# Where the second mamba block's small work stands: three edits to the order of a four-stage kernel

## The chip, the core and the metric

The kernel runs on one core of a Trainium2 chip. Its engines work side by side, each through its own list of instructions in order: TensorE (PE in the profile, with its weight loads as PEld), VectorE (DVE), ScalarE (ACT), GpSimd (POOL) and SyncE (SP), which only issues transfers. They meet through semaphores: an instruction that waits holds up everything behind it on its engine. The metric is the device time of one execution in microseconds (us). Lower is better.

## The reference

Two sequences of 1024 tokens with 512 channels go through four sub-layers, each followed by a residual sum and a layer norm:

```python
x = layernorm(x + L0_attn(x))   # mamba: in-projection, causal conv, recurrence over tokens, gate, out-projection
x = layernorm(x + L0_ffn(x))    # one 512x512 linear product, scaled, with tanh norm clipping
x = layernorm(x + L1_attn(x))   # gated linear recurrence: two branches, conv, two gates, scan, out-projection
x = layernorm(x + L1_ffn(x))    # SiLU-gated FFN with integer weights, 2048 wide
```

The part of the first sub-layer that matters here is this one. `dt` and `dA` have one value per head and token, `B` and `C` 16 values per token:

```python
conv = conv_b + sum(xpad[:, k:k+l] * conv_w[:, k] for k in range(4))
x, B, C = split(silu(conv))
dt = softplus(dt + dt_bias);  dA = exp(dt * -exp(A_log))
h = h * dA_t + (dt_t * x_t) outer B_t;   y_t = h . C_t
```

## The kernel before

The data are float32 (the linear product and the FFN split them into two pieces). The 2048 tokens are cut into four blocks of 512 (`TB`), and each block into four chunks of 128.

**Mamba.** For a block, `head` transposes the tokens (L232, copied out of PSUM at L241 by ScalarE and L243 by VectorE), multiplies out B, C and dt (`pbc`, L353), and prepares their convolution, which the function `mix` finishes: three taps on VectorE (`causal_conv`, L264) and a SiLU on ScalarE (L312). For blocks 1 to 3 `by_rows` then computes softplus and the decays on 64 rows (bias L440, softplus L208 to L219, decays L442 to L450), sends them to DRAM (`since`, `decays`) and transposes the row values back (`ptk` L455, `tk` L456). The constants of the decays, `by_hj`, come by two small transfers on POOL's queue (L108), and `exponents` (L192 to L196) turns A_log into three columns of it.

`opening` is block 0's projection, in an order written out by hand for TensorE, VectorE and ScalarE. It ends with the taps of the last channels (`started_in_psum`, L325) and their SiLU (L329), after which `by_token` transposes the result (`pxt`, L632) and the recurrence starts. `recur` runs the four chunks: products `py` (L655, L663), state `pst` (L673), sums on VectorE (L680, L687, L694), and `pxt`, `dtx` (L634) for the next chunk. `weave` puts steps of other generators between the chunks by a plan: here block 0's gate products (`g`, L336 `pg`, SiLU L705) and steps of block 1's head (`ahead`). Then `gate` (L713 and its squares L715) and block 1's `project` follow: its taps (L264), its copies of the decay rows into PSUM (`pl`, L529), its scans (L535), among the out-projection of the block before (`conclude`, L728). SP loads block 1's decay rows (`L<-decays`) once block 0's last chunk has read the tile `L`.

**The rest.** `linear(b)` is the second sub-layer for one block: transposes, split into two pieces (ScalarE L236, VectorE L237), products `po` (L909), scaling (L913), norms (L915 to L931), update and layer norm (the last on POOL, L257). `branches(b)` begins the third: transposes with copies by ScalarE (L241), products `p` (L960), taps (L982, L264). `linear(2)` and `linear(3)` are woven into `branches(0)`. `recurrence` computes the gates and the scan (L1009 to L1031), `project_back` the out-projection `po` (L1037), its bias `r` (L1042), and the sum into the tokens (POOL, L1043). The FFN (L1111 to L1134) fills the rest.

Outside the hand-written stretches a scheduler sets each engine's order from program order, priorities and its own model of durations. `tc.keep_in_program_order` holds one instruction where the program has it; `tc.high_priority()` lets instructions go ahead of others that are ready.

## Time and profile before

| | us |
|---|---|
| median of three runs | 1141.38 |
| lowest and highest run | 1140.03 and 1142.83 |
| the profiled execution: its time | 1140.83 |
| its span, from the first to the last instruction | 1139.0 |
| TensorE busy in the span | 1116.2 |
| VectorE, ScalarE, POOL busy | 677.6, 466.1, 357.8 |

The span by stages, from the chain that ended last and the timeline: block 0's opening to about 71 us, its recurrence to 97, block 1's projection to 162, blocks 2 and 3 to 431, the linear layer and the first branches to 505, the gated recurrence to 768, then the FFN to the end. The chain follows, from the last instruction backwards, what each step waited for; a row of the timeline is start, duration, engine, line, operation, and in brackets how long the engine had been idle and what ended that. Matmul rows overlap a little at their ends, since the profile models those.

### The profile page before, as it was taken

To read this page: it belongs to the slowest core of one execution; us is meant where nothing else is said; L and a number is where in the kernel's file an instruction comes from. 1 tells how busy PE (TensorE), PEld (TensorE's weight loads), DVE (VectorE), ACT (ScalarE), POOL (GpSimd) and SP (SyncE) were. 2 spreads that over 40 slices of the span, in tenths; PEclk is the share of its full clock that TensorE was granted. 3 is DMA by queue.
4 is the path that set the end of the run, shared out by engine and by line. 5 is a ranking of instruction groups with operands and counts; after the bars stand their busy time and mean duration, and the time that the engine had idled before them with its cause. 6 is when DMAs were issued, how large, how long until landed. Compare 5 with 4: busy or idle time off the path is not lost.

```text
span 1139.0 us, 12263 instructions
## 1 busy us (share of the span) xinstructions
PE 1116.2 (98%) x4610; PEld 681.3 (60%) x4610; DVE 677.6 (59%) x1226; ACT 466.1 (41%) x714; POOL 357.8 (31%) x347
## 2 busy tenths in 40 slices
PE   8999999999999999999999999999999999999996
PEld 5455445545544655654444444448888888888885
DVE  5997895696769676862707237083328765225224
ACT  3352634453453233566654372543223223223224
POOL 1547461573348240556123212237501001001000
PEclk9999999999999999999999999999999999999999
DMA  9004002401210047112000000003601001000001
GB/s 325 13 16 167 1 1 90 167 0 39 111 71 0 38 173 207 75 47 74 1 1 0 1 0 1 0 1 121 184 1 38 1 1 37 1 1 10 28 1 40
DMA packets 32732, 59.22 MB, mean 52 GB/s; under 512 B 11841, under 2 KB 12641, under 8 KB 30105
## 3 DMA queue, kind: packets, MB, share of 16 engines
q1 hardware_dynamic: 31464, 57.94, 14.6%
q8 instruction: 38, 0.62, 0.2%
q10 hardware_dynamic: 976, 0.39, 0.1%
q14 instruction: 30, 0.24, 0.1%
q0 software_dynamic: 224, 0.02, 0.0%
HBM read 49.47 MB, written 8.68 MB: 51 GB/s over the span
## 4 chain that ended last, share of the span: by engine, by line
PE 84%; DVE 10%; ACT 4%; issue 1%; DMA 1%; SPq 0%; DVEq 0%; ACTq 0%
PE pgu L1111 21%; PE p L960 17%; PE po L1134 10%; PE pg L336 9%; PE px L336 7%; PE po L728 6%; PE po L1037 4%; PE py L663 3%; DVE acc L264 2%; PE po L909 2%; DVE L L535 2%; PE pxt L632 1%; PE pt L232 1%; DVE xc L713 1%; PE py L655 1%
## 5 line engine op out<-in xcount | busy, mean ns | idle before, releaser
L1120 DVE SCALAR_TENSOR_TENSOR h<-pgu,L_ffn_up_scale,sg 128x512 f32<-128x512 f32 x64 | 47.9, 749 | 147.7 <-PE pgu L1111 143.5
L336 PE MATMUL px<-xT,w_in 128*128 128x512 f32 x256 | 114.6, 597 | 0.0
L550 POOL TENSOR_TENSOR L<-L,gm 128x512 f32<-128x512 f32 x64 | 93.5, 1490 | 66.9 <-DVE bdec L545 29.3
L728 PE MATMUL po<-w_out,xc 128*128 128x512 f32 x256 | 112.5, 593 | 2.1 <-DVE L L535 2.1
L336 PE MATMUL pg<-xT,w_in 128*128 128x512 f32 x256 | 113.5, 594 | 0.0
L960 PE MATMUL p<-xT,w 128*128 128x512 f32 x256 | 112.1, 592 | 1.4 <-ACT xT L241 1.4
L960 PE MATMUL p<-cv,w 128*128 128x512 f32 x256 | 111.0, 592 | 0.0
L1134 PE MATMUL po<-wd,hh 128*128 128x512 f32 x256 | 101.3, 396 | 0.0
L1111 PE MATMUL pgu<-wF__4423,wg 128*128 128x512 f32 x256 | 101.2, 396 | 0.0
L1134 PE MATMUL po<-wd,hl 128*128 128x512 f32 x256 | 101.0, 394 | 0.0
L1111 PE MATMUL pgu<-lo__4424,wg 128*128 128x512 f32 x256 | 100.7, 394 | 0.0
L1111 PE MATMUL pgu<-lo__4424,wu 128*128 128x512 f32 x256 | 100.7, 393 | 0.0
L1111 PE MATMUL pgu<-wF__4423,wu 128*128 128x512 f32 x256 | 100.7, 393 | 0.0
L1118 ACT ACTIVATE sg<-pgu,L_ffn_gate_scale 128x512 f32<-128x512 f32 x64 | 44.1, 689 | 132.9 <-PE pgu L1111 132.9
L1126 ACT CAST hh<-h 128x512 fp32r<-128x512 f32 x64 | 39.7, 621 | 117.6 <-DVE h L1120 117.4
L728 PEld LDWEIGHTS po<-w_out,xc 128*128 128x128 f32 x256 | 48.4, 190 | 63.1 <-issue 55.5
L960 PEld LDWEIGHTS p<-cv,w 128*128 128x128 f32 x256 | 48.4, 190 | 59.8 <-issue 58.6
L960 PEld LDWEIGHTS p<-xT,w 128*128 128x128 f32 x256 | 48.4, 190 | 58.8 <-issue 55.3
L336 PEld LDWEIGHTS px<-xT,w_in 128*128 128x128 f32 x256 | 47.6, 190 | 57.6 <-issue 56.7
L1241 POOL TENSOR_TENSOR x<-x,r 128x512 f32<-128x512 f32 x12 | 15.2, 1295 | 206.1 <-DVE r L1240 206.1
L336 PEld LDWEIGHTS pg<-xT,w_in 128*128 128x128 f32 x256 | 47.3, 190 | 54.2 <-issue 53.3
L264 DVE SCALAR_TENSOR_TENSOR acc<-xpad,cols,acc 128x512 f32<-128x512 f32 x72 | 67.5, 941 | 18.5 <-ACT acc L306 14.8
(279 smaller groups left out, 1934.5 us busy)
## 6 DMA issues: line engine op xcount, KB each, us to landing
L<-decays SPq DMA_DIRECT2D x12, 1024.0 KB, 8.3
x_mid<-x SPq DMA_DIRECT2D x4, 1024.0 KB, 3.9
x<-x_mid SPq DMA_DIRECT2D x4, 1024.0 KB, 7.2
st<-in_L_ffn_gate_w_dram SPq DMA_DIRECT2D x8, 512.0 KB, 4.7
st<-in_L_ffn_up_w_dram SPq DMA_DIRECT2D x8, 512.0 KB, 3.9
st<-in_L_ffn_down_w_dram SPq DMA_DIRECT2D x8, 512.0 KB, 3.7
x<-_attn_hidden_states_dram SPq DMA_DIRECT2D x3, 1024.0 KB, 16.6
out_dram<-x SPq DMA_DIRECT2D x3, 1024.0 KB, 4.3
```

The lines of the kernel that those rows point to most:

```text
L264: nc.vector.scalar_tensor_tensor(acc, xpad[:, k : k + TB], w[:, k : k + 1], acc, ALU.mult, ALU.add)
L336: nc.tensor.matmul(pm[:n, :], w_in[:, k, lo : lo + n], xT[:, k, :], start=(k == 0), stop=(k == NK - 1),)
L550: nc.gpsimd.tensor_tensor(L[:, h, :], L[:, h, :], st["gm"], ALU.mult)
L663: nc.tensor.matmul(pys[i][hh * HD : (hh + 1) * HD, q, :], dtx[q][:, 2 * i + hh, :], L[:, h, s], start=(first and q == 0), stop=(q == 1), s ...
L728: nc.tensor.matmul(po, xc[:, m, j * P : (j + 1) * P], w_out[:, m, :], start=(m == 0), stop=(m == NX - 1),)
L960: nc.tensor.matmul(pm, w1[:, i, k, m * P : (m + 1) * P], rhs[:, k, :], start=(k == 0), stop=(k == NK - 1),)
L1037: nc.tensor.matmul(po, y[:, k, j * P : (j + 1) * P], w1[:, 4, k, :], start=(k == 0), stop=(k == NK - 1),)
L1111: nc.tensor.matmul(pm, w[g][:, k, cols], x[:, k, :], start=(k == 0 and x is pieces[0]), stop=(k == NK - 1 and x is pieces[-1]),)
L1118: nc.scalar.activation(sg, pgu[0], AF.Silu, scale=gs[:, m : m + 1])
L1120: nc.vector.scalar_tensor_tensor(h, pgu[1], us[:, m : m + 1], sg, ALU.mult, ALU.mult)
L1126: nc.scalar.copy(hh, h)
L1134: nc.tensor.matmul(po[j], x[:, j * P : (j + 1) * P], wd[m // GK][:, m % GK, :], start=(m == 0 and x is h[0]), stop=(m == NF - 1 and x is h ...
```

## The change

Four edits, and line numbers in the text stay those of the kernel before:

1. `opening` no longer runs `mix` of block 1 (its second `next(coming)` goes). The plan of block 0's recurrence becomes (2, 2, 1, 2) over (ahead, g, ahead, g, g, g, ahead): `mix` stands after chunk 0, the decays after chunk 1, `ptk` after chunk 3. The first tap of that `mix` is held in program order.
2. `by_rows` of block 1: the bias L440 is issued ahead of `exponents` and is held in program order; `exponents` is no longer held.
3. The first step of `linear(2)`, its transposes and split, is issued ahead of `branches(0)` rather than after its transposes.
4. The bias `r` of `project_back` (L1042) is issued at high priority.

```diff
-    def causal_conv(acc, xpad, w):
+    def causal_conv(acc, xpad, w, pinned=False):
         for k in range(3):
-            nc.vector.scalar_tensor_tensor(
+            tap = nc.vector.scalar_tensor_tensor(
                 acc, xpad[:, k : k + TB], w[:, k : k + 1], acc, ALU.mult, ALU.add
             )
+            if pinned and k == 0:
+                tc.keep_in_program_order(tap)
...
-        def rest():
-            causal_conv(acc[:n, :], xpad[:n, :], w)
+        def rest(pinned=False):
+            causal_conv(acc[:n, :], xpad[:n, :], w, pinned)
...
-            mix()
+            mix(b == 1)
...
+        bias, _, end, rA, rN = (by_hj[:, i : i + 1] for i in range(5))
+        shifted = nc.vector.tensor_scalar(z, z, bias, None, ALU.add)
         if b == 1:
-            exponents(*(by_hj[:, i : i + 1] for i in range(1, 5)), pinned=True)
-        bias, _, end, rA, rN = (by_hj[:, i : i + 1] for i in range(5))
-        nc.vector.tensor_scalar(z, z, bias, None, ALU.add)
+            tc.keep_in_program_order(shifted)
+            exponents(*(by_hj[:, i : i + 1] for i in range(1, 5)))
...
         later.pop(0)()
-        next(coming)
         for conv in later:
...
-            turns = (ahead, g, g, ahead, g, g)
-            weave(recur(b, H, st), (next(steps, None) for steps in turns), (2, 2, 1, 1))
+            turns = (ahead, g, ahead, g, g, g, ahead)
+            weave(recur(b, H, st), (next(steps, None) for steps in turns), (2, 2, 1, 2))
...
-                    nc.vector.tensor_tensor(r, po, bout, ALU.add)
+                    with tc.high_priority():
+                        nc.vector.tensor_tensor(r, po, bout, ALU.add)
...
-            weave(branches(0, st), itertools.chain(linear(2), linear(3)), (1,) * 8)
+            rest = itertools.chain(linear(2), linear(3))
+            next(rest)
+            weave(branches(0, st), rest, (0,) + (1,) * 7)
```

In the changed program, as built, the instructions stand as follows on each engine; where nothing is said, the order is the one before.

- VectorE at the start: after the first copy L243 come three instructions of block 1's `exponents` (L192, L193, L194 on `by_hj`, the first waiting for the A_log transfer), then the second copy L243. ScalarE: after its first copy L241 comes that group's `exp` (L195), then its second copy L241.
- VectorE in block 0: all taps L325, then `dtx` and chunk 0; `mix`'s three taps after chunk 0's work; L440 to L216 after chunk 1's; the rest of the decays among chunk 2's work; `tk` (L456) among the products L713. `ptk` is TensorE's last instruction before block 1's projection.
- TensorE at `branches(0)`: the 16 transposes of block 2 before the 16 of block 0. ScalarE: three of linear(1)'s squares L915, a split copy L236, the fourth L915, a second L236, the norm L919, two more L236, table load and tanh L923, and then the four copies L241; before it was four L915, L919, L923, two L236, four L241, two L236.
- VectorE in `project_back` of blocks 0 to 2: the four `r` stand together after the last scan L1025 and before the last L1031; before, one stood ahead of that L1031 and three behind it.

## The prediction

> **What bounds the kernel now.** I read the page's busy shares first, then TensorE's waits, then the timeline around each wait.

> ```profile
> PE 1116.2 (98%) x4610; PEld 681.3 (60%) x4610; DVE 677.6 (59%) x1226; ACT 466.1 (41%) x714; POOL 357.8 (31%) x347
> ```

> TensorE is busy 98%: all four edits together can win at most its idle 22.8 us (1139.0 - 1116.2). TensorE's list of waits names the ones in reach:

> ```profile
> PE pxt L632 <- ACT xc L329: 2.4, 1, 2.4
> PE po L728 <- DVE L L535: 2.1, 2, 1.1
> PE po L1037 <- DVE r L1042: 1.7, 1, 1.7
> ...
> PE p L960 <- ACT xT L241: 1.4, 1, 1.4
> ...
> PE po L909 <- DVE wd L237: 0.8, 1, 0.8
> ...
> PE pt L232 <- POOL xpad L976: 0.5, 1, 0.5
> ```

> The first is the opening's end (edits 1, 2), the fourth and sixth stand ahead of branches(0) (edit 3), the third is the bias (edit 4). Now the timeline of the start:

> ```profile
> 4.97 0.56 POOL L108 DMA_DIRECT2D by_hj<-in_L_attn_A_log_dram  x1
> ...
> 8.72 0.69 DVE L243 COPY xT<-pt 128x512 f32<-128x512 f32 x1 [0.18 <-PE pt L232]
> ...
> 9.05 1.93 PE L353 MATMUL pbc<-xT,w_bc 128*48 128x256 f32 x16
> ...
> 12.49 7.13 PE L336 MATMUL px<-xT,w_in 128*128 128x512 f32 x16
> ```

> From 12.49 to 51.5 the rows of TensorE touch each other: what starts late there stays late.

> **Part A, the start: +2.6 us.** Unpinned, block 1's exponents stand between VectorE's two copies L243 and wait for the A_log transfer. The DMA table prices it:

> ```profile
> by_hj<-in_L_attn_A_log_dram POOLq DMA_DIRECT2D x1, 0.2 KB, 6.5
> ```

> Issued at 4.97, it lands at 11.47. L192 to L194 take 0.44 (their twins on 128x16 ran from 9.33 to 9.77). So the second L243 runs 11.9 to 12.6 instead of 8.72 to 9.41; queued behind it, ScalarE's L195 (0.20) and its second copy L241 (0.59) end at 12.7. The product pbc has four k steps of 0.48 and needs a copy for each: the last two end at 13.6 instead of 11.0. Everything up to 51.5 moves by 2.6. Bounds: 0, if it landed before 8.5; 3.3, if it took the 7.2 of the slowest POOL row.
> [...] The row says 6.5, and it decides.

> **Part B, the wait at 71: -1.9.** Block 1's work between the last taps cost VectorE 4.98 (chain pieces from 61.43 to 69.68: L264 1.22, 0.66, 0.66; L440 0.20; L208 0.20; L210 0.12; L211 0.86; L212 1.06). Without it the last tap ends at 70.42 - 4.98 + 2.6 = 68.0, but its SiLU L329 is queued on ScalarE behind the gate L705 of a pg that ended at 67.98 and now ends at 70.6: 70.6 + 0.6 + 0.63 gives 71.85 against TensorE's arrival at 71.35. A wait of 0.5 to 0.6 is left of 2.44, so A and B together are +0.7 at the first py.

> **Part C, where the work goes: +1.6 instead of that +0.7.** The mix (three taps of 0.76) fits into the gap after chunk 0, whose next py comes only after a pg. The decays start after chunk 1's dtx, 85.37 + 0.65 = 86.0. Block 2's rows price them: L440 to the first L216 3.1, six L216 1.87, L217, L219, L442, L443, L444 1.5, exp, scan and memset 0.8, together 7.3. Among them lie chunk 2's L694 1.4, L680 0.35, two L687 1.2 and two dtx 1.3, together 4.2; alternating saves about 0.8 of the waits of one step for the last. So VectorE reaches chunk 3's sums at 86.0 + 7.3 + 4.2 - 0.8 = 96.7, where it now waits for TensorE until 95.38:

> ```profile
> 95.38 0.79 DVE L694 TENSOR_TENSOR xc<-xc,py 128x256 f32<-128x256 f32 x2 [2.32 <-PE py L663]
> ...
> 99.12 9.06 DVE L713 TENSOR_TENSOR xc<-xc,g 128x512 f32<-128x512 f32 x6
> ```

> It is +1.3 there, and `tk` (0.29), now among the L713, makes 1.6. From here the chain of waits runs L713, square L715, ScalarE's xpad and acc, taps L264, scans L535, to the pxt at 161.91, by VectorE and ScalarE alone; TensorE idled 1.05 + 1.02 + 0.65 in that stretch, waiting for them. So 1.6 passes on whole. Bounds: +1.0, if alternating hides 1.4; +3.7, if the slow rows of 61 to 92 return (L212 1.14 for 0.28, L216 0.90 for 0.31, L687 1.67 for 1.06, which add 2.1).
> Covered: the row transfers. `decays` is written about 14 us later, lands near 100, and SP's four loads of L (1 MB each, 4 MB at some 340 GB/s, 12 us) end at 112.5; ScalarE first reads them at 122.54 (pl, L529). Were that cover gone, the excess would count whole. `cdec` goes ahead of them on SP; `ptk` waits for nothing late.

> **Part D, the linear step: +1.0.** Block 2's transposes need no layer norm, so the 0.45 on POOL goes. But look at ScalarE:

> ```profile
> 464.37 1.28 ACT L923 ACT_TABLE_LOAD   x1
> 465.66 0.20 ACT L923 ACTIVATE f<-v 128x4 f32<-128x4 f32 x1
> 465.77 1.05 ACT L236 CAST wu<-pt 128x512 fp32r<-128x512 f32 x2
> 466.72 2.06 ACT L241 COPY xT<-pt 128x512 f32<-128x512 f32 x4
> ```

> TensorE's p L960 waits 1.41 for the first L241. Now all four L236 (0.51 each) stand ahead of it, two of them before the fourth L915: third L915 from 462.63 (0.76), L236, L915 0.73, L236, L919 0.20, two L236, table load 1.28, tanh 0.20, with small gaps 467.87; the first L241 ends at 468.4, not 467.3. It is +1.05. VectorE's wd wait at 496 (0.79) may shrink: part of linear(2)'s split is done earlier, but a layer norm on POOL and the tap behind it start later. I take +1.0; bounds +0.3 (that wait gone) and +1.3.

> **Part E, the bias: 0.** TensorE's 1.66 ends with the first `r`, which frees its bank; it follows the same scan:

> ```profile
> 752.81 1.28 DVE L1025 TENSOR_TENSOR_SCAN hs<-al,last,gx 128x512 f32<-128x512 f32 x1
> 754.01 0.67 DVE L1042 TENSOR_TENSOR r<-po,L_attn_b_out 128x512 f32<-128x512 f32 x1
> 754.59 0.68 DVE L1031 TENSOR_TENSOR y<-y,hs 128x512 f32<-128x512 f32 x1
> ```

> The other three `r` now stand ahead of the last L1031: y comes 3 x 0.62 later, at 757.1. The first po (3.43) needs it for its last quarter, near 757.5; these 0.4 cover it. Bounds 0 and +0.5, if the scan runs long.

> **The sum.** A + B + C is +1.6 in the end, D +1.0, E 0: +2.6. The span becomes 1141.6, the profiled run's 1140.83 becomes 1143.4; that run lay 0.55 below the median, so on the median 1141.38 it is **1144.0**, 0.23% more. By the bounds: low, with A at 0 the 1.6 becomes -1.0, and with D at +0.3 the sum is -0.7: 1140.7; high, A +0.7, C +2.1, D +0.3 and E +0.5 more: 1147.6.
> [...] Part A leaves TensorE idle for 2.6; the profile's 2.44 at 69 left the granted clock at 1.00. [...]

> **The rivals.** A difference under 0.3% (3.4 us) can't be told from none.
> *Slower: the decays overrun chunk 3.* Place: VectorE from 86 to 97, price one for one from where its sums L694 come after TensorE's py (96.0). For it: the slow rows above, all beside POOL's L638, and w_out's scaling (L773, 92.31 to 98.1) is there too. Against: block 2's same chain shows none of them. +2.1: 1146.1. Chance 0.27.
> *By_hj is early enough, or its delay is lost.* For it: VectorE has idle rows before 52. Against: TensorE has none from 12.49, and skips, issued a microsecond earlier, released POOL only at 10.68. C's 1.6 becomes -1.0, D +1.0: 1141.4. Chance 0.13.
> *The edits do what they aim at.* The waits of 1.9, 0.45 + 1.41 and 1.66 go, 5.4 in all: 1136.0. Against: the queues of A, D and E. Chance 0.10.
> *My forecast*, 1144.0: 0.50; its own range is 1142.4 to 1146.0, and 0.14 of it lies above 1144.8, the bound of slower.

> **How the numbers follow.** Slower 0.27 + 0.14 = 0.41; within 0.3% 0.36 + 0.13 = 0.49; faster 0.10. The range, 1139.5 to 1147.5, leaves out the last rival and a tail of the first.

> **What would show it.** A: an idle of about 3 us ahead of L192 on VectorE, released by by_hj, and px at 15.1. B: the wait at pxt under 1. C: VectorE's first L694 of chunk 3 over 1.5 us later than 95.38 with no wait for py before it, and the pxt of block 1 near 163.5. D: p L960 waits over 3 us for L241. E: po L1037 still waits 1.7 for r. I am wrong if L192 waits under 1 us, or if pxt of block 1 comes before 161.9.

## The result and the profile after

| | before | after |
|---|---|---|
| median, six runs of each (us) | 1141.87 | 1146.94 |
| lowest and highest | 1140.03 and 1142.83 | 1144.95 and 1148.12 |
| profiled execution: span | 1139.0 | 1144.8 |
| its mean granted TensorE clock | 0.998 | 0.995 |

The ratio is 1.0045, with a 95% interval from 1.0032 to 1.0058: slower by about 5.1 us. That is inside the range of the prediction, 2.9 us above its number, and on the side of slower, which had 0.41 against 0.49 for no change. Line numbers of the changed kernel are shifted (L336 is L338, L353 is L355, L632 L636, L634 L638, L687 L691, L694 L698, L713 L717, L915 L919, L960 L964, L1031 L1035, L1037 L1041, L1042 L1047); each experiment's rows have its own.

The page of the changed kernel, its busy line and the row of the granted clock in 40 slices:

```profile
PE 1120.3 (98%) x4610; PEld 682.8 (60%) x4610; DVE 678.0 (59%) x1226; ACT 462.6 (40%) x712; POOL 358.6 (31%) x347
...
PEclk8999999999999999999999999999999999999999
```

The same 4610 matrix products took TensorE 1120.3 us, where they took 1116.2. Work that got longer without getting more is a sign to look at the clock, and its first slice is below 9. Then TensorE's waits, in us in total, times, and the longest:

```profile
PE p L964 <- ACT xT L241: 2.7, 1, 2.7
PE pbc L355 <- DVE xT L243: 2.5, 1, 2.5
...
PE po L1041 <- DVE r L1047: 1.7, 1, 1.7
...
PE py L667 <- DVE dtx L638: 0.9, 2, 0.8
...
PE pxt L636 <- DVE dtx L638: 0.4, 1, 0.4
PE po L1041 <- DVE y L1035: 0.3, 1, 0.3
```

The wait of 2.4 at the first `pxt` is down to 0.4. In its place stand a new one of 2.5 at `pbc`, 0.9 at `py`, 0.3 at `y`, and the one at `p` is 2.7 for 1.4. The bias's 1.7 is untouched. Now the start in the timeline (start, duration, engine, line, operation, idle time before it and what ended it):

```profile
7.74 0.69 DVE L243 COPY xT<-pt 128x512 f32<-128x512 f32 x1 [5.04 <-PE pt L232]
...
11.45 0.14 DVE L192 TENSOR_SCALAR by_hj<-by_hj 64x1 f32<-64x1 f32 x1 [3.01 <-DMA by_hj<-in_L_attn_A_log_dram]
...
11.77 0.67 DVE L243 COPY xT<-pt 128x512 f32<-128x512 f32 x1
...
12.50 1.12 PE L355 MATMUL pbc<-xT,w_bc 128*48 128x256 f32 x8 [2.48 <-DVE xT L243]
...
15.17 6.19 PE L338 MATMUL px<-xT,w_in 128*128 128x512 f32 x8
```

VectorE stood 3.01 us before L192 for A_log, the second copy L243 behind it came at 11.77 instead of 8.72, and `px` began at 15.17 instead of 12.49. But eight `px` rows then took 6.19 us, while sixteen took 7.13 before. The table by stretches shows why; its columns are the stretch, its length, the busy time (and number of rows) of PE, PEld, DVE, ACT and POOL, the granted clock, the DMA share and GB/s:

```profile
10.02:12.50 2.48, 0.00 (x1) 0.01 (x1) 1.02 (x6) 0.63 (x2) 0.37 (x2) 1.00 0.92 348
...
13.20:13.40 0.20, 0.20 (x4) 0.00 (x0) 0.00 (x0) 0.00 (x0) 0.00 (x0) 0.96 1.09 430
13.40:13.60 0.20, 0.20 (x2) 0.00 (x0) 0.00 (x0) 0.00 (x0) 0.00 (x0) 0.50 1.19 471
14.00:20.00 6.00, 5.92 (x15) 3.13 (x16) 3.83 (x17) 1.77 (x6) 0.35 (x2) 0.50 1.03 402
...
20.20:20.40 0.20, 0.20 (x2) 0.06 (x1) 0.17 (x2) 0.00 (x0) 0.00 (x0) 0.97 1.05 389
```

The clock was 1.00 through the idle 2.48 us, fell to 0.50 at 13.39 and came back at 20.21: 6.8 us at half speed, soon after the idle time, and never in the kernel before, whose clock is 1.00 in the whole of that stretch.

Following the same instruction in both traces gives the account. How much later than before each began, in us:

| instruction | later by | what is new since the row above |
|---|---|---|
| `px`, first row | 2.68 | the stall at `pbc` |
| `pl` at 51.5 before | 5.17 | 2.49, the halved clock |
| `py` of block 0, first row | 3.16 | -2.01, the wait at `pxt` |
| sums L698 of chunk 3 | 6.06 | +2.90, VectorE late |
| end of the gate L717 | 2.50 | -3.56, faster gate products |
| `pxt` of block 1, its last | 4.18 | +1.68, taps that wait for POOL |
| `p` L964, 505.59 before | 5.04 | +0.86, the linear step |
| first `pgu`, 768.17 before | 5.59 | +0.55, the bias |
| the last instruction | 5.8 | +0.2, behind the last row of every computing engine; not followed up |

### The profile page after: what moved, and what is told of

The parts are those of the page before. It is cut to its first block, busy times and chain, and to the rows that moved or that the text cites. A ratio compares the mean times of both kernels' runs of the same rounds, so it can differ in the third digit from the quotient of the medians.

```text
span 1144.8 us, 12265 instructions
## 1 busy us (share of the span) xinstructions
PE 1120.3 (98%) x4610; PEld 682.8 (60%) x4610; DVE 678.0 (59%) x1226; ACT 462.6 (40%) x712; POOL 358.6 (31%) x347
## 4 chain that ended last, share of the span: by engine, by line
PE 83%; DVE 9%; ACT 4%; issue 1%; POOL 1%; DMA 1%; DVEq 0%; ACTq 0%; POOLq 0%
PE pgu L1119 21%; PE p L964 17%; PE po L1142 10%; PE pg L338 9%; PE px L338 8%; PE po L732 6%; PE po L1041 3%; PE py L667 2%; PE po L913 2%; DVE acc L264 2%; DVE L L540 1%; PE pxt L636 1%; PE pt L232 1%; PE py L659 1%; DVE st L251 1%
## 5 line engine op out<-in xcount | busy, mean ns | idle before, releaser
L338 PE MATMUL px<-xT,w_in 128*128 128x512 f32 x256 | 117.1, 607 | 0.0
L964 PE MATMUL p<-xT,w 128*128 128x512 f32 x256 | 111.8, 592 | 2.7 <-ACT xT L241 2.7
L732 PE MATMUL po<-w_out,xc 128*128 128x512 f32 x256 | 112.5, 593 | 1.8 <-DVE L L540 1.8
L338 PE MATMUL pg<-xT,w_in 128*128 128x512 f32 x256 | 113.5, 594 | 0.0
L964 PE MATMUL p<-cv,w 128*128 128x512 f32 x256 | 111.0, 592 | 0.0
L964 PEld LDWEIGHTS p<-xT,w 128*128 128x128 f32 x256 | 48.4, 190 | 60.8 <-issue 56.0
L964 PEld LDWEIGHTS p<-cv,w 128*128 128x128 f32 x256 | 48.4, 190 | 59.8 <-issue 58.6
L338 PEld LDWEIGHTS px<-xT,w_in 128*128 128x128 f32 x256 | 48.5, 194 | 59.0 <-issue 57.5
L338 PEld LDWEIGHTS pg<-xT,w_in 128*128 128x128 f32 x256 | 47.3, 190 | 54.2 <-issue 53.3
L264 DVE SCALAR_TENSOR_TENSOR acc<-xpad,cols,acc 128x512 f32<-128x512 f32 x72 | 68.0, 948 | 18.4 <-ACT acc L308 12.2
```

The source lines that it names most:

```text
L264: tap = nc.vector.scalar_tensor_tensor(acc, xpad[:, k : k + TB], w[:, k : k + 1], acc, ALU.mult, ALU.add)
L338: nc.tensor.matmul(pm[:n, :], w_in[:, k, lo : lo + n], xT[:, k, :], start=(k == 0), stop=(k == NK - 1),)
L732: nc.tensor.matmul(po, xc[:, m, j * P : (j + 1) * P], w_out[:, m, :], start=(m == 0), stop=(m == NX - 1),)
L964: nc.tensor.matmul(pm, w1[:, i, k, m * P : (m + 1) * P], rhs[:, k, :], start=(k == 0), stop=(k == NK - 1),)
```

## The experiments

Times are medians; a ratio is to the kernel before, run beside it, with its 95% interval. "Edits 1 and 2 held" means them with block 1's `exponents` kept in program order.

| run | what it is | median us | ratio (interval) | `px` from | `pxt` of block 1 | granted clock of its executions |
|---|---|---|---|---|---|---|
| e1_pinned | all four edits, `exponents` held | 1142.13 | 1.0009 (1.0 to 1.0018) | 12.49 | 160.32 | 0.994 to 0.998 |
| e2_fill | the changed kernel, 18 products in the stall | 1146.44 | 1.0049 (1.0035 to 1.0063) | 16.94 | 164.80 | 0.994 to 0.998 |
| e2b_fill9 | the same with 9 | 1145.42 | 1.0031 (1.002 to 1.0043) | 15.62 | 164.06 | 0.994 to 0.998 |
| e5_block | edits 1 and 2 held | 1139.68 | 0.9991 (0.9982 to 1.0) | 12.45 | 160.31 | 0.997 to 0.998 |
| e6_scale | e5_block, scaling of `w_out` moved | 1138.43 | 0.9972 (0.9962 to 0.9982) | 12.43 | 159.21 | 0.997 to 0.998 |
| e8_best | e6_scale, `exponents` earlier | 1138.92 | 0.9977 (0.9968 to 0.9985) | 13.11 | 159.87 | 0.997 to 0.998 |
| e3_linear | the kernel before, edit 3 | 1142.0 | 1.0009 (1.0 to 1.0018) | 13.01 | 161.55 | 0.995 to 0.998 |
| e10_lin | e6_scale, edit 3 | 1140.01 | 0.9993 (0.9984 to 1.0001) | 13.15 | 159.94 | 0.994 to 0.998 |
| e11_linfill | e10_lin, 9 products ahead of `p` | 1139.78 | 0.9989 (0.998 to 0.9998) | 12.97 | 159.73 | 0.997 to 0.998 |
| e4_bias | e5_block, edit 4 | 1141.05 | 0.9995 (0.9986 to 1.0004) | 12.76 | 161.18 | 0.997 to 0.998 |
| e12_copy | e6_scale, copies for `p` ahead | 1147.56 | 1.0058 (1.0045 to 1.0071) | 13.26 | 160.03 | 0.991 to 0.995 |

The granted clock is a mean over the whole execution. It includes the kernel's end: TensorE's last product ends at 1130.1 in the profile of the kernel before and at 1135.7 in the changed kernel's, and the clock is 0.50 from 1135.01 to the end at 1139.0, and from 1139.78 to the end at 1144.8. In the profiles with no other loss that alone makes 0.998 or 0.997; one window of half clock among the products (1.7 us lost, see below) takes off another 0.0015. So 0.996 or less tells of a loss among the products, while 0.997 leaves it open: e3_linear's profiled execution reads 0.997 and has one.

Where nothing was done to the start, `px` began between 12.43 and 13.26, since the first tokens land a little earlier or later (the transposes that wait for them go on at 7.30 in e6_scale and at 8.02 in e10_lin, and `px` begins 5.13 later in both); differences under 0.8 us between two kernels are therefore read between two instructions of a trace, not from the medians.

**The start: stall, and clock.** First, without the float of `exponents`:

```diff
-            exponents(*(by_hj[:, i : i + 1] for i in range(1, 5)))
+            exponents(*(by_hj[:, i : i + 1] for i in range(1, 5)), pinned=True)
```

> All four edits, but block 1's exponents are held in program order again, so that nothing waits for the A_log transfer at the start. Theory (the start cost a stall of 2.7 us and then a halved TensorE clock worth another 2.5): px starts at 12.5 again, the granted clock stays 1.00 from 13 to 21 us, and the whole 5.2 us go: about 0.2 us from the kernel before, 5.2 under the changed kernel. Rival (only the stall belongs to the start; px is slow for another reason): the first px rows stay near 0.77 us each and 2.7 us go, which leaves about 2.5 us more than before.

`px` began at 12.49 again, the clock stayed at 1.00, and `pl` stood at 51.52, 0.01 from its old place: the whole 5.2 us belong to these three floated instructions. In the profiled pair the theory's number came out, 0.2 us over the kernel before (spans 1139.2 and 1139.0). The median was 1.4 us over it; what may make up the difference stands below, at edit 3.

That run takes the stall and the clock away together. To part them, TensorE was kept busy while the stall stayed:

```diff
                     xT[:, k, i * half : (i + 1) * half], start=(k == 0), stop=(k == NK - 1),
                 )
+            if b == 0 and k == 1:
+                for _ in range(18):
+                    nc.tensor.matmul(early[:, :P], ident, ident, start=True, stop=True)
```

> The changed kernel, with 18 small products of the identity into the unused bank of the warm-up put between the two halves of the pbc product, where TensorE waits 2.5 us. The stall stays (VectorE still waits for A_log), TensorE is busy through it. Theory (idling brought the clock down): the granted clock stays 1.00, px starts near 15.0 with rows of 0.45 us, the shift at 51 us is 2.7 in place of 5.2, and the time falls by 2.5 us against the changed kernel. Rival (the clock has nothing to do with the idle time): the clock is 0.50 from 13.4 to 20.2 us as before and the time does not move, or is longer by what the products delay pbc.

The clock stayed at 1.00 and `px` ran at 0.45 us a row, but the products took 4.29 us, not 2.5: the filling outlasted the stall, `px` began at 16.94, and the time shows nothing. So once more with `range(9)`:

> As the run with 18 products, with 9: each took 0.24 us on TensorE there, so 18 outlasted the stall and moved px to 16.94; 9 end near 12.3, before the second half of pbc can start at 12.5. Theory (idling brought the clock down): the granted clock is 1.00 throughout, px starts at 15.1 with rows of 0.45 us, the shift at 51 us is 2.7, and the time is 2.5 us under the changed kernel, some 2.6 us over the kernel before. Rival (the stall costs 5 us by itself): as the changed kernel, some 5 us over.

In that run's timeline of TensorE:

```profile
9.84 1.07 PE L355 MATMUL pbc<-xT,w_bc 128*48 128x256 f32 x8
10.84 2.27 PE L361 MATMUL early<-ident 128*128 128x128 f32 x18
13.04 1.07 PE L355 MATMUL pbc<-xT,w_bc 128*48 128x256 f32 x8
...
15.62 7.13 PE L338 MATMUL px<-xT,w_in 128*128 128x512 f32 x16
```

and in its table of stretches, at the start and near edit 3:

```profile
14.00:20.00 6.00, 5.43 (x21) 2.82 (x20) 3.36 (x15) 2.69 (x7) 0.35 (x2) 1.00 1.03 404
...
468.00:474.00 6.00, 3.82 (x6) 1.75 (x7) 5.09 (x15) 3.56 (x7) 0.00 (x0) 0.76 0.49 175
474.00:480.00 6.00, 6.00 (x22) 3.91 (x22) 5.26 (x15) 2.88 (x5) 0.18 (x1) 0.96 0.00 0
```

Sixteen `px` rows take the 7.13 us of the kernel before, and the clock is 1.00 where it was 0.50. `px` began 3.13 late (the tokens landed later in this execution, where the transposes go on at 8.16, for 7.27 in the changed kernel, and the products kept the second half of `pbc` to 13.04, where its copy was there at 12.40) and `pl` 3.14: nothing is lost behind the stall, where the changed kernel lost 2.49. But this profile alone doesn't part theory and rival: with the tokens late, TensorE would have stood idle only from 10.91 to some 12.46 without the products, 1.55 us, and that might have left the clock alone. The executions part them in part: the changed kernel's six have mean clocks of 0.992 to 0.995, while of the twelve with products eight have 0.996 or more. The median is 1.5 us under the changed kernel's, not 2.5; `px` began 0.45 later than there, which takes part of it, and this profile has a second low stretch, at 468, behind edit 3's wait at `p`.

What settles it lies in all the profiles together. Within each one, the clock changes only at times that are whole multiples of 3.413 us apart: in the changed kernel's profile 6.83 from the fall to the rise and 1119.57 from there to the fall at the end, 2 and 328 times 3.413; in e12_copy's 10.24, 40.96 and 3.42, which is 3, 12 and 1 times. So it goes by windows of that length here, and they lie differently in each execution: counted from its start, the first whole one begins at 1.79 in the kernel before, at 3.14 in the changed kernel and at 2.28 in e12_copy. The table has TensorE's idle time within one window and the granted clock of the next one:

| run | wait in it | window from | idle in it, us | clock in the next |
|---|---|---|---|---|
| e12_copy | `pt`, for POOL | 452.84 | 2.80 | 0.50 |
| e2b_fill9 | `p` | 467.69 | 2.49 | 0.50 |
| the changed kernel | `pbc`, 2.48 | 9.97 | 2.48 | 0.50 |
| e2_fill | `p` | 468.78 | 2.17 | 0.50 |
| e3_linear | `p`, 2.75 | 463.67 | 2.16 | 0.50 |
| e12_copy | `po`, for `wd` | 504.04 | 2.02 | 0.50 |
| e1_pinned | `p`, most of 2.72 | 462.06 | 1.73 | 1.00 |
| the kernel before | `r`, 1.66 | 752.72 | 1.66 | 1.00 |
| the changed kernel | `p`, 2.73 in two windows | 467.36 and 470.77 | 1.29 and 1.44 | 1.00 |
| the kernel before | `pxt`, 2.44 in two windows | 66.64 and 70.05 | 1.31 and 1.14 | 1.00 |

The six with 0.50 are all the falls that the thirteen profiles have before TensorE's last product; 1.73 is the most idle time that any window there had without one. So the six windows with 2.02 us or more were each followed by half a clock, those with 1.73 or less never, and the two waits of over 2.4 that an edge split nearly in half did nothing. In these profiles idle time brings the clock down, and the rival falls; in the changed kernel's profile all of the stall lay in one window.

**Edits 1 and 2 without that cost.** The kernel before with edits 1 and 2 held, none of edits 3 and 4:

> The kernel before with edits 1 and 2 alone (mix and decays kept behind the taps), and block 1's exponents held in program order. Theory (tap relief of 1.9 us, of which VectorE's overload in chunks 2 and 3 gives back 1.0 by block 1's pxt): pxt of block 1 comes near 161.0, 0.9 us before its 161.91, and the time is 0.9 us under the kernel before. Rival (the overload costs its full size, 2.9 us at chunk 3's sums, since nothing later absorbs it): pxt of block 1 near 162.9, 1.0 us slower.

`pxt` of block 1 came at 160.31, 1.6 us earlier than before, and the time is 1.1 us less. `py` came 2.04 earlier (69.41 for 71.45), and of this only 0.44 was given back. The rival, an overload at its full size, falls. Yet VectorE's overload itself is there: the sums of chunk 3 begin 26.25 us after the first `py`, for 23.93 before. In the changed kernel it reads, on VectorE and POOL (POOL's row L721 in a window of its own, 104.8 to 107.4, so that its first sum stands alone):

```profile
95.38 5.68 POOL L777 TENSOR_SCALAR w_out<-w_out,cols 128x512 f32<-128x512 f32 x8
95.46 0.77 DVE L691 SCALAR_TENSOR_TENSOR H<-H,over 128x128 f32<-128x128 f32 x1
...
97.78 0.69 DVE L447 TENSOR_SCALAR work<-turn,by_hj 64x128 f32<-64x128 f32 x1
...
98.99 0.81 DVE L448 TENSOR_SCALAR work<-work,by_hj 64x128 f32<-64x128 f32 x1
...
99.12 1.75 PE L667 MATMUL py<-L,dtx 128*64 128x128 f32 x28 [0.78 <-DVE dtx L638]
...
101.44 0.75 DVE L698 TENSOR_TENSOR xc<-xc,py 128x256 f32<-128x256 f32 x2
...
104.84 2.49 DVE L717 TENSOR_TENSOR xc<-xc,g 128x512 f32<-128x512 f32 x4
105.20 3.26 POOL L721 TENSOR_TENSOR sums<-sums,sq 128x512 f32<-128x512 f32 x1 [4.13 <-ACT sq L719]
...
119.57 1.54 DVE L264 SCALAR_TENSOR_TENSOR acc<-xpad,cols,acc 128x512 f32<-128x512 f32 x2 [2.52 <-POOL xpad L306]
```

Several rows beside POOL's scaling of `w_out` take two to three times their usual 0.30 to 0.34 (L691) and 0.28 to 0.34 (L447, L448); others there, L217 and L219, keep their 0.28. TensorE's `py` waits for `dtx`, and the sums are late. Then the gate gives most of it back. In the kernel before, POOL's sums ran beside five of its last six products, and these took 1.75 each:

```profile
99.48 8.15 POOL L717 TENSOR_TENSOR sums<-sums,sq 128x512 f32<-128x512 f32 x5 [1.35 <-ACT sq L715]
```

In the changed kernel POOL stood still from 101.06 to 105.20, waiting for the late squares; two products had it idle beside them, and the next four kept their 0.68 too (2.49 for four, which overlap a little). Three of these ran beside POOL's first sum, and here POOL lost the time: that sum took 3.26, where the later ones took 1.26 to 1.60. Only the last two products took 1.55 and 1.75. Why POOL gave way there and VectorE before is not shown. The gate ends early, until POOL's sums, also late, hold up the `xpad` rows and with them the next taps (2.52). To test that the scaling makes the rows slow, it was moved to follow chunk 0:

```diff
+            def scale():
+                for m in range(NX):
+                    tc.keep_in_program_order(nc.gpsimd.tensor_scalar(
+                        w_out[:, m, :], w_out[:, m, :], normw[:, m : m + 1], 1.0,
+                        ALU.mult, ALU.mult
+                    ))
+                yield
-            turns = (ahead, g, ahead, g, g, g, ahead)
-            weave(recur(b, H, st), (next(steps, None) for steps in turns), (2, 2, 1, 2))
-            for m in range(NX):
...
+            scaled = scale()
+            turns = (scaled, ahead, g, ahead, g, g, g, ahead)
+            weave(recur(b, H, st), (next(steps, None) for steps in turns), (3, 2, 1, 2))
```

> Edits 1 and 2 with block 1's exponents held, and POOL's scaling of w_out moved from behind the whole recurrence to behind chunk 0 (about 80 to 86 us), where VectorE has little to do; to be read against the run with edits 1 and 2 alone. Theory (the slow decay rows of chunk 2 and 3, L216 at 0.79 and L447 to L449 at 0.6 to 0.8, are slow because POOL scales w_out beside them): they fall to 0.2 to 0.35, chunk 3's first sums come 2 to 2.5 us earlier and wait for TensorE again, and block 1's pxt comes up to 1.0 us earlier. Rival (POOL's sums of squares set block 1's taps, and these start when the gate's squares do): rows fall, but pxt of block 1 moves by less than 0.3.

```profile
74.91 6.66 POOL L776 TENSOR_SCALAR w_out<-w_out,cols 128x512 f32<-128x512 f32 x8
...
90.75 0.34 DVE L691 SCALAR_TENSOR_TENSOR H<-H,over 128x128 f32<-128x128 f32 x1
...
92.28 0.27 DVE L447 TENSOR_SCALAR work<-turn,by_hj 64x128 f32<-64x128 f32 x1
...
94.56 0.75 DVE L698 TENSOR_TENSOR xc<-xc,py 128x256 f32<-128x256 f32 x2
...
112.69 2.34 DVE L264 SCALAR_TENSOR_TENSOR acc<-xpad,cols,acc 128x512 f32<-128x512 f32 x3 [2.52 <-POOL xpad L306]
```

With the scaling at 74.91, L691 takes 0.34 and L447 0.27; the mix's three taps, now beside it, take 3.61 for 2.97, in time that VectorE had to spare. Some L216 stay slow (1.07 and 0.79, at 88.2 and 89.5, beside POOL's L642). Against the run with edits 1 and 2 held, the sums of chunk 3 come 1.10 earlier (2 to 2.5 were expected), POOL's sums end 1.09 earlier and `pxt` of block 1 comes 1.10 earlier: what VectorE gains there passes on one for one, and the theory's 1.0 at `pxt` holds. The rival would have had under 0.3. This is the fastest kernel of the study, 0.28% under the kernel before (interval 0.18% to 0.38%).

Then block 1's `exponents` were issued right behind the first layer's own, on top of this:

> The run with w_out's scaling moved, and block 1's exponents issued right behind the first layer's own, where VectorE stands idle for 2.9 us at 9.9 (they wait for A_log until 11.4 and have nothing urgent behind them until 12.8). Theory: no stall at the start, px at 12.5, and 0.5 us less on VectorE among the decays: between 0 and 0.5 us under the run with the scaling moved, some 1.5 us under the kernel before. Rival (the wait for A_log holds up z and the softplus behind it): px or its taps come later, and it is slower than that run.

It gained nothing: from `px` to `pxt` of block 1 it took 146.76 us, the run before it 146.78. Its median is 0.5 higher, and its `px` began 0.7 later; in this profile the first copy L243 already came at 8.46 (7.84 before), so the tokens were late, and the floated rows, at 13.47, had no part in it.

**Edit 3, the linear step.** Alone on the kernel before:

> The kernel before with edit 3 alone (the first linear step ahead of the branches). Theory (ScalarE's four split copies now stand before the four copies that p waits for): p waits 2.7 us for the copy in place of 1.4, POOL's 0.45 goes, and by the end the time is 0.7 to 0.9 us more. Rival (the earlier split pays it back at the wd wait, 0.8 us): 0 to 0.1 us more.

`p` waited 2.75 and POOL's 0.45 was gone, as in the changed kernel, whose ScalarE shows the queue:

```profile
467.43 0.57 ACT L236 CAST wu<-pt 128x512 fp32r<-128x512 f32 x1
...
468.52 0.57 ACT L236 CAST wu<-pt 128x512 fp32r<-128x512 f32 x1
...
469.09 1.07 ACT L236 CAST wu<-pt 128x512 fp32r<-128x512 f32 x2
470.18 1.28 ACT L927 ACT_TABLE_LOAD   x1
...
471.59 2.03 ACT L241 COPY xT<-pt 128x512 f32<-128x512 f32 x4
```

From the first of these transposes to the first `p` of the convolved branch, 52.46 us passed; 50.82 before. That is 1.64, more than 0.9: in this execution the granted clock was 0.92 from 462 to 468 and 0.79 from 468 to 474. The median is 1.2 over the kernel before. So edit 3 was put on the quieter base of the run with the scaling moved, and then the idle time was filled:

> The run with w_out's scaling moved, with edit 3 (the first linear step ahead of the branches) added; its base has no idle time of TensorE over 1.7 us, and its runs lie within 0.9 us of each other. Theory (edit 3 costs its wait, and in a part of the executions a lower clock behind it, by where the idle 2.7 us fall against the clock's windows): 0.9 us over the base in executions with a granted clock of 0.998, and about 1.7 us more in others with 0.996 or less; median 0.9 to 2.6 over the base, spread over 2 us. Rival (only the wait counts): 0.9 us over the base, spread as in the base.

```diff
                 xT = transposed(rp, b, X, by_act=True)[0]
+                if b == 0:
+                    spare = bank("spare")
+                    for _ in range(9):
+                        tc.keep_in_program_order(
+                            nc.tensor.matmul(spare[:, :P], ident, ident, start=True, stop=True)
+                        )
                 yield
```

> As the run with edit 3 added, with 9 small products of the identity into an unused bank (2.1 us) behind the branches' transposes, where TensorE waits 2.7 us for ScalarE's copy. Theory (the idle time lowers the clock): the wait stays as time, the granted clock stays 1.00 between 450 and 485 us, the spread shrinks to that of the base, 0.9 us over the base. Rival (the clock falls for another reason, the copies' or the products' own): the spread stays over 2 us.

In both the same stretch took 51.65, 0.80 over the base's 50.85. Without the filling the runs spread over 3.3 us (1139.29 to 1142.61): eight of twelve with a mean clock of 0.998 and spans from 1137.4 to 1138.4, four with 0.994 to 0.997 and spans up to 1140.7. With it the wait left to TensorE is 0.70, every run has 0.997 or 0.998, and they spread over 1.1 us (1139.29 to 1140.38):

```profile
462.98 2.17 PE L982 MATMUL spare<-ident 128*128 128x128 f32 x18
465.86 3.70 PE L969 MATMUL p<-xT,w 128*128 128x512 f32 x8 [0.70 <-ACT xT L241]
```

Useless work made the kernel steadier, and no slower (medians 1139.78 and 1140.01). This pair is the cleaner test of the filling: 2.6 of the 2.7 us would have lain in one window (from 463.26), and with 0.70 of it left idle the clock stayed at 1.00. In e10_lin's own profile an edge split the wait into 1.41 and 1.29, and the clock stayed up without help; its four slower executions were not profiled. The theory holds in kind. In size the median of e10_lin rose by 1.6 over the base, of which the trace gives 0.8 to the wait and 0.7 to `px`, which began that much later in the profiled execution; the base was timed in another batch, where the kernel before read 1141.54 for 1140.94 here, so the 1.6 is rough. The first experiment fits: it kept edit 3, and only four of its eleven runs had 0.998.

The other way about, ScalarE's copies for `p` ahead, by high priority for the branches' transposes:

```diff
-                xT = transposed(rp, b, X, by_act=True)[0]
+                with tc.high_priority():
+                    xT = transposed(rp, b, X, by_act=True)[0]
```

> The run with w_out's scaling moved, without edit 3, but the branches' transposes and copies of block 0 to 3 at high priority, so that ScalarE's four copies for p stand ahead of the linear step's squares and split copies. Theory (p's wait of 1.4 and the 0.45 for POOL's rows are ScalarE's order alone): p starts up to 1.4 us earlier, up to 1.4 us faster than the base. Rival (the split copies and the tanh chain come later, and po waits for them instead): no change or slower.

Slower by 0.58% (0.45% to 0.71%), on the rival's side and far beyond its size. The priority moved the transposes on TensorE as well, and there they wait in order for the layer norm on POOL, 4.7 us in three waits. `po` also waited 2.1 for `wd`, as the rival has it, where the base waits 0.8. And the idle time cost clock: 0.50 from 456.25 to 466.49 and from 507.45 to 510.87, which is 6.8 us lost (in the slowest of its five executions, 1150.55):

```profile
PE pt L232 <- POOL x L257: 4.7, 3, 1.7
```

**Edit 4, the bias.** On edits 1 and 2 held:

> Edits 1 and 2 with block 1's exponents held, and edit 4 (the bias at high priority), without edit 3; to be read against the run with edits 1 and 2 alone. Theory (the first r still follows the same scan, and y comes three r later): TensorE's wait for r stays 1.7, a new wait for y of 0.3 stands behind it, 0.3 us slower than without edit 4. Rival (the wait for r shortens): up to 1.7 us faster.

```profile
754.08 2.84 PE L1041 MATMUL po<-w,y 128*128 128x512 f32 x6 [1.66 <-DVE r L1047]
757.21 11.43 PE L1041 MATMUL po<-w,y 128*128 128x512 f32 x26 [0.29 <-DVE y L1035]
...
753.36 1.86 DVE L1047 TENSOR_TENSOR r<-po,L_attn_b_out 128x512 f32<-128x512 f32 x3
755.41 0.69 DVE L1047 TENSOR_TENSOR r<-po,L_attn_b_out 128x512 f32<-128x512 f32 x1 [0.19 <-POOL x L1048]
756.01 1.14 DVE L1035 TENSOR_TENSOR y<-y,hs 128x512 f32<-128x512 f32 x1
```

The wait for `r` is 1.66, as it was, and the first `po` runs out of `y` at its last quarter. From this `po` to the first `pgu` it is 13.99 us for 13.43 without edit 4: 0.56, where 0.3 was expected and 0.29 shows as a wait. The fourth `r` waits 0.19 for its buffer (POOL's sum frees it), and the last product for `y` took 1.14, not 0.68.

## Why the prediction was right, and where not

| part | predicted | measured, profiled pair |
|---|---|---|
| A, the start | +2.6 | +5.17: stall 2.68, clock 2.49 |
| B, the wait at `pxt` | -1.9 | -2.01, 0.44 left |
| C, decays, at `pxt` of block 1 | +0.9 (1.6 in place of 0.7) | +1.02 |
| D, the linear step | +1.0 | +0.86 |
| E, the bias | 0 | +0.55 |
| sum | +2.6 | +5.6, and 0.2 at the end |

**A** was right in mechanism and in its stall: the idle 3.01 before L192, released by `by_hj`, and `px` at 15.17 for 15.1. The step that failed stands behind the sum, which has no price for the clock: "the profile's 2.44 at 69 left the granted clock at 1.00". One row of one execution was taken for what such an idle time always does. The runs show that it depends on where the idle time falls. 2.48 us at 10, all in one window, brought the clock down for 6.8 us in the profiled execution. All six executions of the changed kernel have mean clocks of 0.992 to 0.995, so each lost some; how much of it at `pbc` and how much at `p`, a mean doesn't tell. The row that the forecast trusted was one of the lucky ones: the 2.44 straddles an edge at 70.05, 1.31 before it and 1.14 behind. Over the three batches of runs (76), the kernel before has executions at 0.998 with spans of 1138.1 to 1139.9, and executions at 0.995 and 0.996 with 1140.5 to 1142.9, while the four kernels with edits 1 and 2 held and ScalarE's order at `p` as before (e5_block, e6_scale, e8_best, e4_bias), whose wait at `pxt` is 0.4, have none under 0.997. That it is this wait that does it in the kernel before is argued from these lists and from the windows; no profile of the kernel before caught it.

What the fall takes can be read in the windows: 13.39 to 20.21 is two of 3.41, and 468 to 480 in the run with 9 products lost 0.24 x 6 + 0.04 x 6 = 1.7 us, half of one. None of the six windows ahead of a fall was idle throughout: 2.02 out of 3.41 were enough, and 1.73 were not. Behind the stall two windows were low, 3.4 us of clock; 2.49 of it came after `px` had begun, the rest before.

**B** was right to 0.1. The wait left is put down to `dtx`, not to ScalarE's SiLU.

**C** came out right by two errors that cancel. The forecast had the slow rows stay away; they came back, and the sums of chunk 3 were 2.9 late, where the forecast had 0.6 over `py` and the rival "the decays overrun chunk 3" 2.7. So the rival had the place right, and its price there. But the step "1.6 passes on whole", which both shared, failed: the gate's products kept their speed where POOL had slowed them before, and gave most of it back, and POOL's sums, not "VectorE and ScalarE alone", then set the next taps. The loads of `L` stayed covered, as forecast: the queues moved 351 GB/s from 95.6 to 109.0 in the kernel before (some 340 in the forecast), and in the changed kernel, where SP issued the loads from 104.09, 340 GB/s from 104.1 to 118.0; ScalarE first read `L` at 126.72 there. C cost 1.02 in the changed kernel and 0.44 in e5_block, since L448 and L449 took 0.6 less there. That `exponents` is held is not the reason: e4_bias holds it and has the long rows (26.84 from `py` to the sums, for 26.83 in the changed kernel), e2_fill doesn't and has the short ones (26.25, as in e5_block). What decides between the two is not settled.

**D** was right in its queue and its cost in one execution, though the wait was 2.7 and not over 3; what it adds through the clock was not in it. **E** had its mechanism right and its cover too small by 0.5: the bound of +0.5 was the value. Neither rival of a gain has anything for it.

The number: 1144.0 plus 2.5 for the clock and 0.55 for E is 1147.0, close to the 1146.94 measured. That closeness is partly luck, since the kernel before moved too, from 1141.38 in three runs to 1141.87 in six, and C's sum is right by accident. So is the place inside the range: of the 3.6 us that the high bound adds, 2.1 are for a late VectorE and none for the clock. A small misreading in A's bound: the slowest row on POOL's queue is 7.3 (`cbr`), not 7.2.

## What to carry to other kernels

An idle time of TensorE had two prices here: itself, and a lower clock behind it, by how much of it fell into one of the clock's windows (2.02 of 3.41 us were enough, 1.73 were not). One profile showed the one without the other (2.44 us in the kernel before with the clock at 1.00), so read the mean clocks of several runs before you leave the clock out of a sum, and where a wait of 2 us or more can't be removed, try a few useless products in an unused bank: here 9 of 0.24 us kept the clock at 1.00 (e11_linfill, every run 0.997 or 0.998, where four of e10_lin's twelve had 0.994 to 0.997). Before small work is moved "behind" something, look at what the scheduler does with the instructions that are no longer held: three of them, far from the edit's place, cost more here than all the rest of the change. And a wait removed from one engine is worth what the next engine lets through: here that was POOL, once with VectorE's rows beside it slow (L691 0.77 for 0.34) and once by its own queue (2.52 us ahead of the taps).
